# Both ends of layer 0: bias tables, loads, the last token chunk and the branch weights moved to other places in the order

## The chip, the cores and the metric

The kernel runs on one core of a Trainium2 chip. The metric is device microseconds of one execution. Before the change the median of three runs was 2273.14 us (2273.03 to 2274.25). The profiled execution spans 2274.0 us; all times inside it are counted from its start.

A core has a matrix engine (PE, with PEld for the loading of its weights), a vector engine (DVE), a scalar engine for activations and copies (ACT), a general engine (POOL) and a queue that mostly issues transfers (SP). ACT can issue transfers too; its queue then works through them in order, between its other instructions.

## The reference, cut to what matters

The input x has shape (2, 128, 64, 64) in float32: two images of 64 x 64 places with 128 channels. Layer 0 is a group norm, then a neighbourhood attention block: every place attends to a 7 x 7 window, in 4 heads, with a bias table per head, followed by a projection and a small chain of three linear maps with layer norms:

```python
x = x + _L0_conv_ref(_gn(x), ...)
t = _to_tokens(x)
t = t + _L1_attn_ref(_ln_t(t))
t = t + _L1_ffn_ref(_ln_t(t), sigma, phi, M_u, M_phi_plus, M_phi_minus, log_weights, gumbel)
```

Layer 1 is an attention of all 4096 tokens of an image with each other (the diagonal left out), and then a spectral filter: long causal convolutions in four branches of different length, of which a hard choice over `log_weights + gumbel` picks one. The chosen weights (`wt`, `seg`), a mixed matrix `mu` of short lags and the fourth root of `sigma` are small quantities that the filter needs only after most of the first attention.

## The kernel before, in words

**Layer 0, in bands.** The two images are cut into 16 bands of 8 rows (512 places), band k being image b, group g. A band's work is cut into named pieces: `p.*` (group norm `p.xg`, transposition to tokens `p.tok`, layer norm `p.bn` to `p.zT`, then `p.q`, `p.k`, `p.v` and their copies), four units `u0` to `u3` of the window attention (scores `S`, bias and row minimum `t`, exponential `e`, transposition `T`, copy `c`, product with the values `V`), `r.*` and `t.*` (the rest of the block), and `k.*`. The pieces `k.*` prepare the tokens of image 0 for layer 1 while image 1 is worked on: `k.a` transposes, `k.tt` copies, `k.bn` takes statistics, `k.pw` raises to the power -1/2, `k.z` normalizes on POOL, `k.b` and `k.cm` transpose back. Each band of image 1 handles one chunk of 512 tokens; the last band, k = 15, the last chunk.

**What sets the order.** `PLAN` gives each piece a time in a period of 2300 units, one period per band. All pieces, with the extra events for the tables and the weights, are sorted by that time and recorded in that order; inside `manual_schedule` the order of PE, DVE, ACT and POOL is kept as written. For the first two bands the preparing pieces follow the list `FIRST` instead, which also places the group norm (`gn`), the products for the q, k, v biases (`w`, kept by `wd`), the flips of the bias rows `f0` to `f3` (a PE product on the rows `rev`, and an ACT copy into `base`) and the tables (`tab` on POOL, `tab0` to `tab3` on DVE, each `mask` minus `base`). The queue of SP is not held to the written order.

**Loads at the start.** SP loads image 0 (`xa[0]`), the weights, the bias rows in 8 large pieces (ACT issues 8 small ones for head 0), the window masks, and image 1 (`xa[1]`). Between layer 0 and its attention, values go through memory: `p.vc` stores v to `vd`, and `windows` loads the windows `vw` back.

**Completion semaphores.** In the built program every transfer signals one of eight completion semaphores in turn, and an issue waits until an earlier user of the same semaphore has landed. The wait stands on the queue that issues.

**The end of layer 0 and the attention.** What the last bands have left when image 1's last unit is done is put into the list `later`. The program then enters layer 1: PSUM is handed over from layer 0's pools, `branch_weights` computes the choice, `mu` and the root of sigma, and `attention(0, fill)` begins. Its loop runs over pairs of token chunks; per pair it makes scores (`weights`: PE product, on the diagonal a DVE addition of `ndiag`, an ACT exponential), products `own` and `other`, and turned exponentials (`turned`). At every step it calls `fill()`, which takes one step from generators: first urgent ones (what follows a finished chunk), then, in order, `drain` (the list `later`, three pieces a step), `filters`, and `tokens` of image 1. Instructions of this part may be moved by the scheduler, as far as dependences and its own estimates allow.

Lines to follow below (as in the profile before): L188 transposes of z or of normalized tokens, L248/L252 flip and its copy, L257 tables, L326 transposes of xg or rb, L331 linear maps, L405 ACT's half of a normalization, L414 DVE's half, L435 xg, L459 kT, L508 scores, L521 bias and minimum, L531 exponentials, L544 transposes of them, L655 y, L661 relu of y on POOL, L705 the last step of a token chunk, L892/L899 scores and exponentials of the big attention, L920 own, L945 other, L1058 the root of sigma, L1096/L1098 `mu`.

Of the kernel before, what the change touches and what calls it, by code (L numbers as in the profile page):

```python
# [20 lines left out]
HEADS, DH, KW = 4, 32, 7  # L21
# [21 lines left out]
RPR = NTAB + 1  # L43
# [25 lines left out]
PERIOD = 2300  # L69


FIRST = (
    "gn p.xg0 p.xg1 p.tok0 p.tok1 w f0 p.bn0 p.bn1 f1 p.pw0 p.pw1 p.zd0 p.nb0 p.za0 p.tr0 f2 p.zd1 p.nb1 p.za1 p.tr1 f3"
    " wd p.zT0 tab p.v0 p.q0 p.k0 p.zT1 p.vc0 p.qT0 tab0 p.kT0 p.v1 p.k1 p.q1 p.vc1 p.kT1 p.qT1 tab1 tab2 tab3"
).split()
PHW = P + TH

# [15 lines left out]
def kernel(  # L93
# [16 lines left out]
    nc = tc.nc  # L110
# [12 lines left out]
    xa = [xp.tile([P, T], F32, tag=f"xa{b}", name=f"xa{b}") for b in range(NB)]  # L123
    xin = x.rearrange("b c h w -> b c (h w)")
    for c in range(4):
# [10 lines left out]
    mask = space[:, HEADS * NTAB * NTAB : HEADS * NTAB * NTAB + 6 * KEYS].rearrange("p (c k) -> p c k", k=KEYS)  # L136
# [8 lines left out]
        out=flip, in_=flip, compare_op=ALU.not_equal, fill=1.0, base=1 - QT * QT, pattern=[[0, 2], [1, QT * QT]],  # L145
# [73 lines left out]
    with l0a:  # L219
# [21 lines left out]
        tab = big.tile([P, 6, HEADS, KEYS], F32, name="tab")  # L241
# [38 lines left out]

        nc.gpsimd.memset(rev[:, 0].rearrange("p n m -> p (n m)"), 0.0)
        nc.gpsimd.memset(rev[:, HEADS - 1, NTAB], 0.0)
        for r in range(QT):
            lo = 6 - min(r, 6)
            src = bass.AP(
                rpb_pad.tensor, (RPR + r - 6) * RPW + 50, [[1, QT], [RPW, (HEADS - 1) * RPR - r // 7], [1, NTAB]]
            )
            rows_ = rev[r * QT : (r + 1) * QT].rearrange("p h n m -> p (h n) m")
            nc.sync.dma_start(out=rows_[:, RPR : HEADS * RPR - r // 7], in_=src)
            src = bass.AP(rpb_pad.tensor, (lo + r - 6) * RPW + 50, [[1, QT], [RPW, RPR - lo], [1, NTAB]])  # L290
            nc.scalar.dma_start(out=rows_[:, lo:RPR], in_=src)
        nc.sync.dma_start(out=mask, in_=nc.inline_tensor(_window_masks(), "window_masks").ap())
        wg = w_sb
        cb = wp.tile([P, 5], F32, name="cb")
        C_Q, C_K, C_V, C_1, C_3 = range(5)
# [174 lines left out]
        @piece("p.vc")  # L470
        def _(t, b, g):
            v = ap.tile([P, 4, P], F32, tag="v", name="v")
            nc.scalar.copy(v.rearrange("p j c -> p (j c)"), t["pv"])
            for i, c in enumerate(TILES):
                nc.sync.dma_start(
                    out=vd[b][g * QT : (g + 1) * QT, c * QT : (c + 1) * QT, :],
                    in_=v[(i % 2) * 64 : (i % 2 + 1) * 64, i // 2, :],
                )
            if b == 0 and g == 1:
                for c in range(4):  # L480
                    nc.sync.dma_start(out=xa[1][:, c * 1024 : (c + 1) * 1024], in_=xin[1, :, c * 1024 : (c + 1) * 1024])
            if g:
                windows(b, g - 1)
            if g == NG - 1:
                windows(b, g)
# [290 lines left out]
        for k, (b, g) in enumerate(order):  # L776
            t = {}
            for name, at in PLAN.items():
                if name[0] == "k" and b == 0:
                    continue  # L780

                at = FIRST.index(f"{name}{k}") - 1000 if k < 2 and name[0] == "p" else at + k * PERIOD
                events.append((at, k, name, lambda f=pieces[name], t=t, b=b, g=g: f(t, b, g)))
        for name, f in (
            ("gn", lambda: [None for _ in group_norm(0)]), ("w", weights), ("wd", weights_kept),
# [7 lines left out]
        rest_ = behind()  # L793
        for i in range(4):
            events.append((150 + 350 * i, None, "", lambda: next(rest_)))

        gn1 = group_norm(1)
        for i in range(7):
# [26 lines left out]
            for k, n in want:  # L825
                upto[k] = max(upto[k], rest(k, n))
        whole = [n == len(mine[k]) for k, n in enumerate(upto)]
        now, later = [], []
        for at, k, name, f in events:
            if name == "t.add":  # L830
                early = at <= last or whole[k]
            elif name[:1] in ("r", "t"):
                early = name in mine[k][: upto[k]]
            else:
                early = True
            (now if early else later).append(f)
        engines = mybir.EngineType
        with tc.manual_schedule(engines={engines.PE, engines.DVE, engines.Activation, engines.Pool}):
            for f in now:
# [12 lines left out]
    with ap_:  # L852
# [196 lines left out]
        def branch_weights():  # L1049

            lw = sp.tile([P, NBR], F32, tag="lw", name="lw")
            gu = sp.tile([P, NBR], F32, tag="gu", name="gu")
            nc.sync.dma_start(out=lw, in_=log_w.partition_broadcast(P))
            nc.sync.dma_start(out=gu, in_=gumbel.partition_broadcast(P))
            nc.sync.dma_start(out=sg, in_=sigma.partition_broadcast(P))
            quarter = sp.tile([P, KF], F32, tag="quarter", name="quarter")
            nc.gpsimd.memset(quarter, 0.25)
            nc.gpsimd.tensor_tensor(sg, sg, quarter, ALU.pow)  # L1058

            z = sp.tile([P, NBR], F32, tag="z", name="z")  # L1060
            nc.vector.tensor_tensor(z, lw, gu, ALU.add)
            m = sp.tile([P, 1], F32, tag="zm", name="zm")
            nc.vector.tensor_reduce(m, z, AX.X, ALU.max)
            nc.vector.tensor_scalar(z, z, m, None, ALU.subtract)
            ys = sp.tile([P, NBR], F32, tag="ys", name="ys")
            tot = sp.tile([P, 1], F32, tag="tot", name="tot")
            nc.scalar.activation(ys, z, AF.Exp, bias=0.0, scale=1.0, accum_out=tot)
            nc.vector.reciprocal(tot, tot)
            nc.vector.tensor_scalar(ys, ys, tot, None, ALU.mult)
            nc.vector.tensor_reduce(m, ys, AX.X, ALU.max)  # L1070

            oh = sp.tile([P, NBR], F32, tag="oh", name="oh")
            nc.vector.tensor_scalar(oh, ys, m, None, ALU.is_equal)
            seen = sp.tile([P, NBR], F32, tag="seen", name="seen")
            nc.vector.tensor_copy(seen[:, 0:1], oh[:, 0:1])  # L1075
            for i in range(1, NBR):
                nc.vector.tensor_tensor(seen[:, i : i + 1], seen[:, i - 1 : i], oh[:, i : i + 1], ALU.max)
            for i in range(NBR - 1, 0, -1):
                nc.vector.tensor_tensor(oh[:, i : i + 1], seen[:, i : i + 1], seen[:, i - 1 : i], ALU.subtract)

            for j in range(NBR):
                nc.vector.tensor_copy(seg[:, j : j + 1], seen[:, NBR - 1 - j : NBR - j])
            nc.vector.tensor_tensor(wt, oh, ys, ALU.subtract)
            nc.vector.tensor_tensor(wt, wt, ys, ALU.add)

            mixed(mu, m_u)

        def mixed(dst, src):
            dst2 = dst.rearrange("p k e -> p (k e)")
            for i in range(NBR):  # L1090
                st = sp.tile([P, 4, P], F32, tag="st", name="st")
                n = src.shape[1]
                nc.sync.dma_start(out=st[:, 0:n], in_=src[i].rearrange("k d e -> d k e"))
                st2 = st[:, 0:n].rearrange("p k e -> p (k e)")
                if i == 0:
                    nc.vector.tensor_scalar(dst2, st2, wt[:, 0:1], None, ALU.mult)  # L1096
                else:
                    nc.vector.scalar_tensor_tensor(dst2, st2, wt[:, i : i + 1], dst2, ALU.mult, ALU.add)  # L1098
# [83 lines left out]

            return fill, urgent

        branch_weights()
        def drain():

            rings[:] = [(ps_m, "bank")] * 2
            for i, f in enumerate(later):
                f()  # L1190
                if i % 3 == 2:
                    yield
            l0.close()
            tp1 = ap_.enter_context(tc.tile_pool(name="l1_t1", bufs=1, side="right"))
            tt[1] = tp1.tile([P, NT, P], F32, name="tt1")
            tok[1] = tp1.tile([P, NT, P], F32, name="tok1")
            cm[1] = tp1.tile([P, T], F32, name="cm1")
            yield

        steps = [drain(), filters(), tokens(1, bank)]  # L1200
        fill, left = filler(0, steps)
        attention(0, fill)
        for gen in steps:
# [156 lines left out]
def _window_masks():  # L1360

    import numpy as np

    def seen(offset):

        q, k = np.arange(QT)[:, None], np.arange(WN)[None, :]
        lo = np.clip(offset + q - 3, 0, WN - KW)
        return (k >= lo) & (k < lo + KW)

    m = np.zeros((2, QT, QT, 6, WN, WN), np.float32)  # L1370
    for ci in range(6):
        rows_ = seen((0, 6, 3)[ci // 2])
        for ab in range(2):
            cols = seen(((0, 6), (3, 3))[ci % 2][ab])
            m[ab, :, :, ci] = np.where(rows_[:, None, :, None] & cols[None, :, None, :], 0.0, -MASKED)
    return m.reshape(P, 6, KEYS)
# [77 lines left out]
```

## Time and profile before

| stretch (us) | what happens | PE busy | granted PE clock |
|---|---|---|---|
| 0 to 12 | image 0 loads, group statistics | 0.66 | 1.00 |
| 12 to 25 | first bands' norms, bias rows arrive | 7.50 | 1.00 |
| 25 to 44 | flips, v, q, k of two bands, tables | 14.22 | 1.00 |
| 44 to 60 | first scores of band 0 | 15.71 | 0.57 |
| 60 to 140 | bands in steady work | 74.53 | 0.98 |
| 140 to 260 | the same | 119.84 | 1.00 |
| 260 to 340 | the last bands of image 1 | 75.92 | 1.00 |
| 340 to 350 | the last units | 7.74 | 0.83 |
| 350 to 367 | hand-over to layer 1 | 9.74 | 0.70 |
| 367 to 377 | first products of attention 0 | 9.33 | 1.00 |
| 377 to 860 | attention 0 with fills | 472.23 | 1.00 |
| 860 to 900 | from attention 0 to 1 | 37.08 | 0.91 |
| 900 to 2274 | attention 1, convolution | 1349.48 | 0.99 |

PE is the engine that the whole program waits for: 96% of the span. A table row is to be read as follows: busy PE near the length of the stretch means that only less PE work would shorten it, and a gap means that PE waited for someone. The granted clock is the share of full speed that the throttle allowed; 0.5 is its low state.

In lines of the profile, each row is: start, busy time, engine, line, operation, tile written, tile read, shapes, number of instructions, and in brackets the idle time of the engine before it and what ended it. A float32 product shows as two PE records.

### The profile page before, as it was taken

Reading aid. Unit: us, or ns where it says so; the run is one execution under the profiler, and the core shown is the slowest. Engines: PE = TensorE matmul, PEld = TensorE weight load, DVE = VectorE, ACT = ScalarE, POOL = GpSimd, SP = SyncE. Lnnn points to the kernel's source line nnn. Section 1 sums busy time; section 2 is a strip of 40 time slices with the busy share of each in tenths; the row PEclk is TensorE's granted clock in tenths of the full one; section 3 lists DMA queues with packets and bytes.
Section 4 is the critical chain, followed back from the end, with each engine's and each line's share of the span. In section 5 each row is a group of like instructions: output and inputs, shape, how many; then the busy total and the mean of one; then the engine's idle time right before and its main releaser. Section 6 shows DMA issues by size and latency. Waiting matters only on the chain.

```text
span 2274.0 us, 31748 instructions
## 1 busy us (share of the span) xinstructions
PE 2194.0 (96%) x11908; PEld 1355.6 (60%) x11908; DVE 936.9 (41%) x3047; ACT 784.2 (34%) x1911; POOL 275.9 (12%) x354
## 2 busy tenths in 40 slices
PE   6999998999999999999999979999999999999998
PEld 3677764444444444544544436776776777767777
DVE  4799984333443336533333433222223232232323
ACT  2889883222332233222222223223223232232222
POOL 3377874200000000000000000000000000000000
PEclk8999998999999999999999989999999999999999
DMA  4222213021000015100000033222122121212101
GB/s 120 62 61 61 61 49 50 5 70 47 24 19 5 24 47 150 42 24 15 9 24 23 23 91 91 51 58 53 43 58 52 44 58 39 58 42 55 40 10 74
DMA packets 180858, 109.76 MB, mean 48 GB/s; under 512 B 32225, under 2 KB 165857, under 8 KB 180194
## 3 DMA queue, kind: packets, MB, share of 16 engines
q1 hardware_dynamic: 179466, 107.65, 18.4%
q8 instruction: 94, 1.54, 0.3%
q14 instruction: 58, 0.48, 0.1%
q10 hardware_dynamic: 1240, 0.09, 0.1%
HBM read 73.09 MB, written 34.60 MB: 47 GB/s over the span
## 4 chain that ended last, share of the span: by engine, by line
PE 86%; DVE 6%; POOL 4%; DMA 1%; ACT 1%; issue 1%; SPq 0%; POOLq 0%; DVEq 0%; ACTq 0%
PE acc L1278 25%; PE pc L1267 13%; PE own L920 10%; PE bank L892 9%; PE other L945 8%; PE bank L906 4%; PE bank L331 2%; PE py L1305 2%; PE bank L188 2%; PE bank L1037 2%; PE bank L544 2%; PE bank L1005 2%; PE bank L1141 1%; PE bank L508 1%; DVE ln_st L377 1%
## 5 line engine op out<-in xcount | busy, mean ns | idle before, releaser
L1268 DVE COPY y<-pc 128x512 f32<-128x512 f32 x320 | 221.6, 692 | 358.9 <-PE pc L1267 355.1
L899 ACT ACTIVATE e<-bank 128x512 f32<-128x512 f32 x288 | 171.8, 597 | 566.1 <-PE bank L892 434.1
L892 PE MATMUL bank<-cm 128*128 128x512 f32 x576 | 299.6, 604 | 3.9 <-DVE seen L1075 3.9
L1267 PE MATMUL pc<-ct,ut 64*128 64x512 f32 x1280 | 287.6, 599 | 5.9 <-issue 5.9
L1278 PE MATMUL acc<-y,mpl 128*128 128x256 f32 x1280 | 292.1, 382 | 0.0
L1278 PE MATMUL acc<-y,mmi 128*128 128x256 f32 x1280 | 288.0, 379 | 0.0
L1278 PEld LDWEIGHTS acc<-y,mpl 128*128 128x128 f32 x1280 | 238.1, 190 | 59.4 <-issue 29.6
L1278 PEld LDWEIGHTS acc<-y,mmi 128*128 128x128 f32 x1280 | 242.6, 190 | 32.7
L1268 ACT COPY y<-pc 128x512 f32<-128x512 f32 x320 | 204.3, 638 | 94.8 <-PE pc L1267 94.8
L920 PE MATMUL own<-et,tok 128*128 128x512 f32 x448 | 228.1, 596 | 3.5 <-DVE part L909 3.5
L945 PE MATMUL other<-e,tok 128*128 128x512 f32 x448 | 229.0, 593 | 0.9 <-DVE xa L959 0.9
L909 DVE CUSTOM_DVE_ANT_0 et<-bank,one 128x512 f32<-128x512 f32 x224 | 145.5, 688 | 166.9 <-PE bank L906 166.9
L1267 PEld LDWEIGHTS pc<-ct,ut 64*128 64x128 f32 x1280 | 121.9, 188 | 152.7 <-issue 147.5
L1284 ACT COPY ob<-acc 128x256 f32<-128x256 f32 x40 | 23.8, 595 | 431.2 <-PE acc L1278 431.2
L920 PEld LDWEIGHTS own<-et,tok 128*128 128x128 f32 x448 | 84.2, 190 | 112.5 <-issue 70.1
L945 PEld LDWEIGHTS other<-e,tok 128*128 128x128 f32 x448 | 85.3, 191 | 108.4 <-issue 106.7
L892 PEld LDWEIGHTS bank<-cm 128*128 128x128 f32 x576 | 96.8, 194 | 76.1 <-issue 47.0
L1317 DVE TENSOR_TENSOR xa<-py,xa 128x512 f32<-128x512 f32 x32 | 22.1, 691 | 281.4 <-PE py L1305 281.4
L906 PEld LDWEIGHTS bank<-ident,e 128*128 128x128 f32 x896 | 103.9, 142 | 55.3 <-issue 48.0
L160 POOL TENSOR_TENSOR ln_rs<-ln_rs,mhalf 128x4 f32<-128x4 f32 x24 | 24.3, 1012 | 878.2 <-DVE ln_rs L159 878.2
L531 ACT ACTIVATE p<-p,mn 128x196 f32<-128x196 f32 x256 | 114.4, 449 | 15.7 <-DVE mn L521 15.1
L906 PE MATMUL bank<-ident,e 128*128 128x128 f32 x896 | 117.5, 274 | 0.0
(200 smaller groups left out, 2340.5 us busy)
## 6 DMA issues: line engine op xcount, KB each, us to landing
ut<-us SPq DMA_DIRECT2D x80, 256.0 KB
us<-ub SPq DMA_DIRECT2D x64, 256.0 KB
vw<-vd SPq DMA_DIRECT2D x256, 49.0 KB
ct<-gs SPq DMA_DIRECT2D x160, 72.0 KB
ct<-gs SPq DMA_DIRECT2D x160, 64.0 KB
gs<-ub SPq DMA_DIRECT2D x20, 256.0 KB
xa<-in_x_dram SPq DMA_DIRECT2D x8, 512.0 KB
vd<-v SPq DMA_DIRECT2D x128, 32.0 KB
```

Source lines behind the costliest of these rows:

```text
L188: nc.tensor.transpose(ps[:, j * P : (j + 1) * P], src[:, j, :], ident)
L331: nc.tensor.matmul(pl, lhsT=wg[:, lo : lo + P], rhs=zT, start=True, stop=True)
L531: nc.scalar.activation(p, p, AF.Exp, bias=t[name + "mn"][:, h : h + 1], scale=-1.0, accum_out=t["den"][:, u, h : h + 1],)
L892: nc.tensor.matmul(ps, lhsT=cm[b][:, n * P : (n + 1) * P], rhs=cm[b][:, chunk(c)], start=True, stop=True)
L899: nc.scalar.activation(e, ps, AF.Exp, bias=0.0, scale=ASCALE, accum_out=part[:, n, c : c + 1])
L906: nc.tensor.transpose(pt[:, k * P : (k + 1) * P], es[k][:, m * P : (m + 1) * P], ident)
L909: nc.vector.tensor_tensor_reduce(et, pt, one, 1.0, 0.0, ALU.mult, ALU.add, part[:, n, a : a + 1])
L920: nc.tensor.matmul(own, lhsT=tok[b][:, n, :], rhs=e, start=first, stop=last)
L945: nc.tensor.matmul(other, lhsT=tok[b][:, 4 * CHUNKS[a] + j, :], rhs=es[j], start=(j == 0), stop=(j == 3))
L1267: nc.tensor.matmul(pc, lhsT=ut[fp, b, par, :], rhs=cv_[fp], start=True, stop=True)
L1268: (nc.scalar.copy if f else nc.vector.tensor_copy)(y[:, 4 * f : 4 * f + 4, :, par, b * 2 * FB + q : (b + 1) * 2 * FB : 2], pc.rearrange("p ...
L1278: nc.tensor.matmul(acc, lhsT=(mmi if l else mpl)[:, k, :], rhs=y[:, 1::2, k, ::-1, :] if l else y[:, 0::2, k, :, :], start=(l == 0 and k = ...
```

## The change: what it does and what it is for

It has four parts.

1. **Written order of the start.** `FIRST` is rewritten: both bands' normalizations come before the bias flips, `f0` follows `p.zT0`, `f1` follows `p.tr1`, `f2` and `f3` come after band 0's q, k, v, and POOL's tables after these. `p.xg2` is put into the list early. The placing rule now takes every name in `FIRST`, not only the first two bands.
2. **Loads of the start.** The masks are loaded ahead of the bias rows; two of the eight large pieces of bias rows (r = 2 and 5) are issued by ACT. The load of image 1 leaves SP's queue: ACT issues its four pieces, as an event at time 1000 of band 0, so that they keep out of the bias rows' way.
3. **The last chunk of tokens.** The `k` pieces of the last band are taken out of the written order and put at the head of `later`, so that they become steps between the attention's products.
4. **Branch weights.** `branch_weights` becomes a generator with `yield`s: its first loads are issued where it stood, and the rest are steps of the fill, after `drain`.

The arithmetic is the same before and after.

```diff
--- before.py
+++ after.py
@@ -70,8 +70,8 @@
 
 
 FIRST = (
-    "gn p.xg0 p.xg1 p.tok0 p.tok1 w f0 p.bn0 p.bn1 f1 p.pw0 p.pw1 p.zd0 p.nb0 p.za0 p.tr0 f2 p.zd1 p.nb1 p.za1 p.tr1 f3"
-    " wd p.zT0 tab p.v0 p.q0 p.k0 p.zT1 p.vc0 p.qT0 tab0 p.kT0 p.v1 p.k1 p.q1 p.vc1 p.kT1 p.qT1 tab1 tab2 tab3"
+    "gn p.xg0 p.xg1 p.tok0 p.tok1 w p.bn0 p.bn1 p.pw0 p.pw1 p.zd0 p.nb0 p.za0 p.tr0 p.zd1 p.nb1 p.za1 wd p.xg2 p.zT0 f0"
+    " p.tr1 f1 p.v0 p.q0 p.k0 p.zT1 p.vc0 p.qT0 tab0 p.kT0 f2 f3 tab p.v1 p.k1 p.q1 tab1 p.vc1 p.kT1 p.qT1 tab2 tab3"
 ).split()
 PHW = P + TH
 
@@ -280,16 +280,16 @@
 
         nc.gpsimd.memset(rev[:, 0].rearrange("p n m -> p (n m)"), 0.0)
         nc.gpsimd.memset(rev[:, HEADS - 1, NTAB], 0.0)
+        nc.sync.dma_start(out=mask, in_=nc.inline_tensor(_window_masks(), "window_masks").ap())
         for r in range(QT):
             lo = 6 - min(r, 6)
             src = bass.AP(
                 rpb_pad.tensor, (RPR + r - 6) * RPW + 50, [[1, QT], [RPW, (HEADS - 1) * RPR - r // 7], [1, NTAB]]
             )
             rows_ = rev[r * QT : (r + 1) * QT].rearrange("p h n m -> p (h n) m")
-            nc.sync.dma_start(out=rows_[:, RPR : HEADS * RPR - r // 7], in_=src)
+            (nc.scalar if r % 3 == 2 else nc.sync).dma_start(out=rows_[:, RPR : HEADS * RPR - r // 7], in_=src)
             src = bass.AP(rpb_pad.tensor, (lo + r - 6) * RPW + 50, [[1, QT], [RPW, RPR - lo], [1, NTAB]])
             nc.scalar.dma_start(out=rows_[:, lo:RPR], in_=src)
-        nc.sync.dma_start(out=mask, in_=nc.inline_tensor(_window_masks(), "window_masks").ap())
         wg = w_sb
         cb = wp.tile([P, 5], F32, name="cb")
         C_Q, C_K, C_V, C_1, C_3 = range(5)
@@ -476,9 +476,6 @@
                     out=vd[b][g * QT : (g + 1) * QT, c * QT : (c + 1) * QT, :],
                     in_=v[(i % 2) * 64 : (i % 2 + 1) * 64, i // 2, :],
                 )
-            if b == 0 and g == 1:
-                for c in range(4):
-                    nc.sync.dma_start(out=xa[1][:, c * 1024 : (c + 1) * 1024], in_=xin[1, :, c * 1024 : (c + 1) * 1024])
             if g:
                 windows(b, g - 1)
             if g == NG - 1:
@@ -779,7 +776,7 @@
                 if name[0] == "k" and b == 0:
                     continue
 
-                at = FIRST.index(f"{name}{k}") - 1000 if k < 2 and name[0] == "p" else at + k * PERIOD
+                at = FIRST.index(f"{name}{k}") - 1000 if f"{name}{k}" in FIRST else at + k * PERIOD
                 events.append((at, k, name, lambda f=pieces[name], t=t, b=b, g=g: f(t, b, g)))
         for name, f in (
             ("gn", lambda: [None for _ in group_norm(0)]), ("w", weights), ("wd", weights_kept),
@@ -793,6 +790,11 @@
         rest_ = behind()
         for i in range(4):
             events.append((150 + 350 * i, None, "", lambda: next(rest_)))
+        def second():
+            for c in range(4):
+                nc.scalar.dma_start(out=xa[1][:, c * 1024 : (c + 1) * 1024], in_=xin[1, :, c * 1024 : (c + 1) * 1024])
+
+        events.append((1000, None, "", second))
 
         gn1 = group_norm(1)
         for i in range(7):
@@ -825,7 +827,8 @@
             for k, n in want:
                 upto[k] = max(upto[k], rest(k, n))
         whole = [n == len(mine[k]) for k, n in enumerate(upto)]
-        now, later = [], []
+
+        now, later, chunk_ = [], [], []
         for at, k, name, f in events:
             if name == "t.add":
                 early = at <= last or whole[k]
@@ -833,7 +836,8 @@
                 early = name in mine[k][: upto[k]]
             else:
                 early = True
-            (now if early else later).append(f)
+            (chunk_ if name[:1] == "k" and k == bands[-1] else now if early else later).append(f)
+        later = [*chunk_, *later]
         engines = mybir.EngineType
         with tc.manual_schedule(engines={engines.PE, engines.DVE, engines.Activation, engines.Pool}):
             for f in now:
@@ -1053,6 +1057,7 @@
             nc.sync.dma_start(out=lw, in_=log_w.partition_broadcast(P))
             nc.sync.dma_start(out=gu, in_=gumbel.partition_broadcast(P))
             nc.sync.dma_start(out=sg, in_=sigma.partition_broadcast(P))
+            yield
             quarter = sp.tile([P, KF], F32, tag="quarter", name="quarter")
             nc.gpsimd.memset(quarter, 0.25)
             nc.gpsimd.tensor_tensor(sg, sg, quarter, ALU.pow)
@@ -1067,6 +1072,7 @@
             nc.scalar.activation(ys, z, AF.Exp, bias=0.0, scale=1.0, accum_out=tot)
             nc.vector.reciprocal(tot, tot)
             nc.vector.tensor_scalar(ys, ys, tot, None, ALU.mult)
+            yield
             nc.vector.tensor_reduce(m, ys, AX.X, ALU.max)
 
             oh = sp.tile([P, NBR], F32, tag="oh", name="oh")
@@ -1077,13 +1083,16 @@
                 nc.vector.tensor_tensor(seen[:, i : i + 1], seen[:, i - 1 : i], oh[:, i : i + 1], ALU.max)
             for i in range(NBR - 1, 0, -1):
                 nc.vector.tensor_tensor(oh[:, i : i + 1], seen[:, i : i + 1], seen[:, i - 1 : i], ALU.subtract)
+            yield
 
             for j in range(NBR):
                 nc.vector.tensor_copy(seg[:, j : j + 1], seen[:, NBR - 1 - j : NBR - j])
             nc.vector.tensor_tensor(wt, oh, ys, ALU.subtract)
             nc.vector.tensor_tensor(wt, wt, ys, ALU.add)
 
+            yield
             mixed(mu, m_u)
+            yield
 
         def mixed(dst, src):
             dst2 = dst.rearrange("p k e -> p (k e)")
@@ -1182,7 +1191,6 @@
 
             return fill, urgent
 
-        branch_weights()
         def drain():
 
             rings[:] = [(ps_m, "bank")] * 2
@@ -1197,7 +1205,9 @@
             cm[1] = tp1.tile([P, T], F32, name="cm1")
             yield
 
-        steps = [drain(), filters(), tokens(1, bank)]
+        chosen = branch_weights()
+        next(chosen)
+        steps = [drain(), chosen, filters(), tokens(1, bank)]
         fill, left = filler(0, steps)
         attention(0, fill)
         for gen in steps:
```

## The prediction

> **What bounds the kernel now.** I read the page first, then busy time by stretch, then the instructions in order of time at the two ends of layer 0, and last the two programs' built orders.
>
> ```profile
> PE 2194.0 (96%) x11908; PEld 1355.6 (60%) x11908; DVE 936.9 (41%) x3047; ACT 784.2 (34%) x1911; POOL 275.9 (12%) x354
> ```
>
> PE (TensorE) is busy for 96% of 2274.0 us, so 80 us is all that any reordering could win. In the table by stretch (columns: stretch, sum, busy time of PE, weight loads, DVE, ACT, POOL, then granted clock, DMA share, GB/s) PE is full in the middle and loose at the ends:
>
> ```profile
> 12.00:25.00 13.00, 7.50 (x22) 4.81 (x22) 6.90 (x33) 2.56 (x5) 4.07 (x7) 1.00 0.97 154
> 25.00:44.00 19.00, 14.22 (x40) 7.50 (x40) 4.54 (x12) 5.63 (x12) 8.19 (x15) 1.00 0.23 74
> 140.00:260.00 120.00, 119.84 (x1844) 88.48 (x1843) 114.08 (x592) 107.53 (x332) 94.56 (x116) 1.00 0.22 61
> 350.00:367.00 17.00, 9.74 (x23) 5.08 (x24) 7.53 (x39) 2.43 (x8) 13.96 (x15) 0.70 0.00 0
> ```
>
> From 12 to 44 PE idles 10.3 us, from 350 to 367 7.3 us; after that it loses little. What is gained at an end stays, because the middle is bound by PE's own work. At the start:
>
> ```profile
> 22.50 1.67 PE L248 MATMUL bank<-cm,flip 64*128 64x400 f32 x2 [3.38 <-DMA cm<-in_rpb_pad_dram]
> 24.21 0.49 ACT L252 COPY tok<-bank 128x400 f32<-128x400 f32 x1 [4.56 <-PE bank L248]
> 24.60 0.81 ACT L405 ACTIVATE z<-bank,ln_nb,ln_rs 128x128 f32<-128x128 f32 x2
> 25.12 1.25 PE L188 MATMUL bank<-ident,z 128*128 128x128 f32 x4 [0.94 <-ACT z L405]
> 43.30 0.94 PE L326 MATMUL bank<-ident,xg 128*128 128x128 f32 x4 [2.59 <-DVE xg L435]
> 44.17 0.70 PE L508 MATMUL bank<-kT,qT 32*64 32x196 f32 x16
> ```
>
> The bias rows land late; flip f1 waits for them, its ACT copy waits for f1, and behind that copy on the in-order ACT queue stands band 0's normalization (24.60), whose input (ln_nb) was ready at 18.55. The first scores come at 44.17. At the seam:
>
> ```profile
> 349.36 3.15 POOL L705 TENSOR_SCALAR tok<-tt,kmv,krs 128x128 f32<-128x128 f32 x4
> 353.44 1.51 POOL L661 TENSOR_SCALAR y<-y 128x512 f32<-128x512 f32 x1
> 354.98 0.30 DVE L377 BATCH_NORM_STATS2 ln_st<-y 128x6 f32<-128x128 f32 x1 [6.99 <-POOL y L661]
> 357.39 1.12 DVE L655 SCALAR_TENSOR_TENSOR y<-bank,ln_rs,add 128x128 f32<-128x128 f32 x4
> 358.66 6.16 PE L892 MATMUL bank<-cm 128*128 128x512 f32 x10 [3.92 <-DVE seen L1075]
> 359.02 2.93 POOL L1058 TENSOR_TENSOR sg<-sg,quarter 128x16 f32<-128x16 f32 x1
> 362.96 0.41 DVE L394 SCALAR_TENSOR_TENSOR ln_nb<-ln_mv,ln_rs 128x4 f32<-128x4 f32 x1 [4.38 <-POOL ln_rs L385]
> 366.73 1.12 PE L920 MATMUL own<-e,tok 128*128 128x512 f32 x2 [1.91 <-ACT e L899]
> ```
>
> POOL's last token chunk (3.15) holds y, DVE's statistics of y hold L655, the last reader of layer 0's PSUM, and the attention's first products wait for that. Then the power of sigma (2.93) holds POOL's ln_rs, DVE stands 4.38, and the diagonal and exponentials come late.
>
> **What the skill says.** "DMA: Bandwidth & Descriptors", Issuing engines are not separate DMA queues: transfers started by ACT and SP share the engines, so another issuer saves only issue time; Anatomy of one DMA puts any semaphore wait on the issuing sequencer. The trace agrees: SP stood 4.6 us before a bias load for v_sb's landing. "ScalarE: Activation LUTs", What ACT_TABLE_LOAD costs: 1283 ns for the load; here 1.28 (at 12.02). "TensorE: Matmul & The Clock Gate", Part 1: half clock after about 3.4 us of idling. The trace agrees in kind: from 350 to 367 the granted clock was 0.70.
>
> **The start.** The built order gives ACT both za before any copy, but the table load now stands at za0 with its wait, so 18.55 + 1.28 + 0.81 puts tr0 at 20.7 instead of 25.12. PE then has tr0 1.25, f0 1.64, tr1 1.25, f1 1.64: v0 at 26.5 instead of 32.89. The bias rows should land in time for f1 (24.9): they landed at 22.4 by the trace's completion events, and the mask now goes ahead of them (588 KB, about 1.4 us by the 1.28 us between landings of 512 KB chunks). v0 to q1 took 7.8 us, f2 and f3 between them add 3.3: at these half-clock durations k1 ends near 36.8, at the durations of the warm stretch near 33.0. Then kT1 0.88, two tables 1.45 (two of the four now come earlier), statistics 1.18: first score reduction at 36.4 to 40.3 instead of 45.36. I take **7.0 us earlier**. xg of band 2 (0.73) lies in DVE's idle time before kT, POOL's tables beside PE; both cost nothing.
>
> **The cost of moving xa[1].** Its four issues move from SP at 18.44, where nothing waited, to ACT, in the built order right behind band 2's za (52.88) and ahead of unit 1's exponentials (53.66). Issuing is 4 x 0.43 = 1.7 us, but each also waits for an earlier transfer that used its completion semaphore: the built program makes them wait for the 4th, 8th and 12th window load (vw), and the fourth for the second xa piece. SP starts the window loads at 45.59, one each 0.77, landing 2.5 after the issue; moved up by the same 7 the 12th lands at 49.7, while ACT gets there at 46.7. The second piece, issued near 46.7 and landing 3 to 4 later (the first load took 4.0), frees the fourth at 50 to 51. So ACT stands about 4.3 us, with 1.7 (no waits) and 6 as bounds. Queued behind are unit 1's four exponentials, and unit 1's transposes on PE (55.97) need them: 4.0 of it shows. PE idling that long would also go to half clock for a window or so: 1.2 (0 to 2). About 0.4 comes back in PE's 5.5 idle us from 60 to 140. Start, net: 7.0 - 4.0 - 1.2 + 0.4 = **2.2 us gained**.
>
> **The seam.** POOL loses krs and the 3.15; y is ready at 351.8 instead of 354.95. In the built order y's statistics and ln_nb also stand no longer ahead of L655, which then only needs PE's w2, freed from behind the token transposes (350.5): L655 ends near 351.8, the attention's first products start near 352.0 instead of 358.66. Sigma's power moves behind ln_rs, so nothing holds the diagonals; the first own product follows the five products, near 356.4 (warm) to 358.6 (half clock) instead of 366.73. But the last chunk now stands early among the products: its transposes (k.b) come four products after k.a, and their input needs ACT's copy, DVE's statistics (behind mu, which waits for m_u's last pieces, 2.55 us after issue), then POOL: sigma 2.93, y 1.50, krs 1.27, tok 4 x 0.79. By my count tok is ready from 361.9 to 364.2 while PE is there at 360.2: a **new wait of about 3 to 4 us**. PE then reaches the end of the fourth own product (373.74 before) at 367.9, 5.8 earlier; 1.3 off for half clock gives **4.5** (bounds 2 and 9.5, without the wait). The other branch steps are tiny DVE operations beside PE. The chunk's two PE groups (0.88) only change place. Fills: in the built order batch 1's tokens still end inside attention 0, a few steps later, so nothing is left exposed after it.
>
> **Sum:** 2273.1 - 2.2 - 4.5 = 2266.4; I take 2266.5.
>
> **Rivals.** (A) As above, both ends pay in part: 2266.5, chance 0.53 (0.44 of it beyond 0.2%). (B) The ACT wait is absorbed and the token wait hidden: 7.0 + 9.5 less half a microsecond, about 2257; for it, ACT is busy only half of 44 to 60; against it, both waits are in the built order. 0.18. (C) One end gives everything back, for instance the ACT wait and half clock take all of the 7.0 and the seam keeps 2: about 2271, no difference. For it, the trace's clock drops after each hole. 0.19. (D) Slower: ACT stands 6 and PE runs 2 longer on half clock against a start gain of only 5 (loss 3), and at the seam the token wait exceeds what is won: 2276 or more. Against it, the removed waits are large and certain. 0.10.
>
> **Numbers.** The range 2256.5 to 2273.5 leaves out the better half of B and D, 0.19. Faster 0.44 + 0.18 = 0.62; same 0.09 + 0.19 = 0.28; slower 0.10.
>
> **What would show it.** First scores near 35 to 38; ACT idle before unit 1's exponentials, put down to DMA; first attention product near 352 less what the start won; PE waiting for tok on POOL inside the first four own products. Wrong would be: ACT going through its issues in 2 us, no tok wait, the first bias flips waiting on DMA again (mask ahead of the rows), or idle time at the end of attention 0 (820 to 880) growing.

## The result and the profile after

The changed kernel takes 2264.5 us (median of four runs, 2263.27 to 2266.85), the kernel before 2273.55 us beside it: a ratio of 0.9961, 95% interval 0.9944 to 0.9978, so 9 us or 0.4% faster. The predicted time was 2266.5. The profiled execution spans 2263.3 us. Lines of the start and the seam have numbers lower by 3 in this kernel (L505 is L508 of before), those of the attention higher by 4 (L896 is L892). Busy time and instructions by engine:

```profile
PE 2187.7 (97%) x11908; PEld 1354.1 (60%) x11908; DVE 940.2 (42%) x3047; ACT 785.3 (35%) x1911; POOL 277.3 (12%) x354
```

PE's busy time fell from 2194.0 to 2187.7 with the same 11908 products, which is less time at half clock (PE was busy for 64.2 us at half clock before and for 53.2 after); the rest of the gain is idle time. So the 80 us of idle time were not all that a reordering could win, as the prediction took them to be. The granted clock of 1.00 in the first rows, before and after, is no measurement: the first clock record of the traces stands at 37.7 us before and at 30.1 after. Until then products take the times of half clock (the eight records of a value product, L465, 2.08 us at 32.89 before and 1.05 at 37.94), and the two sums at half clock count them so. Where the gain went is read from the table by stretch (columns as before):

```profile
12.00:25.00 13.00, 8.76 (x30) 6.04 (x30) 7.54 (x35) 3.87 (x7) 3.85 (x6) 1.00 0.44 25
25.00:44.00 19.00, 16.10 (x72) 9.95 (x70) 8.66 (x33) 6.50 (x16) 11.69 (x19) 0.90 0.16 40
44.00:60.00 16.00, 9.57 (x82) 5.60 (x80) 5.27 (x26) 6.46 (x22) 0.53 (x1) 0.50 0.56 180
140.00:260.00 120.00, 119.84 (x1846) 88.76 (x1845) 114.30 (x597) 108.00 (x333) 94.10 (x115) 1.00 0.22 61
350.00:367.00 17.00, 11.85 (x36) 5.68 (x37) 11.20 (x49) 4.75 (x16) 16.72 (x18) 0.93 0.57 65
377.00:860.00 483.00, 476.62 (x1581) 233.96 (x1579) 191.29 (x641) 136.24 (x346) 30.30 (x33) 1.00 0.10 33
```

The stretch from 25 to 44 is fuller (14.22 before), but from 44 to 60 PE is busy for 9.57 us instead of 15.71, all of it at half clock: what the start won is lost there. The half clock itself is older than the hole: it begins at 40.4, behind a wait of 2.90 us for DVE (L759, at 39.89), as it began at 44.5 in the kernel before behind one of 2.59. The hand-over gained 2.1, and from 377 to 860, a stretch that the prediction left alone, PE is busy for 4.4 us more (472.23 before), which is idle time gone.

**The start came as drawn, and then a hole opened.** In order of time, PE and then ACT in the kernel after:

```profile
20.28 1.25 PE L188 MATMUL bank<-ident,z 128*128 128x128 f32 x4 [2.95 <-ACT z L405]
...
25.76 2.08 PE L465 MATMUL bank<-w_sb,zT 128*128 128x128 f32 x8
...
35.47 0.59 PE L505 MATMUL bank<-kT,qT 32*64 32x196 f32 x16
```

```profile
45.92 0.37 ACTq L795 DMA_DIRECT2D xa<-in_x_dram  x1
46.23 0.45 ACT L405 ACTIVATE z<-bank,ln_nb,ln_rs 128x128 f32<-128x128 f32 x1
47.02 6.89 ACTq L795 DMA_DIRECT2D xa<-in_x_dram  x3
53.95 0.46 ACT L528 ACTIVATE p<-p,mn 128x196 f32<-128x196 f32 x1 [7.28 <-DMA vw<-vd]
```

The first scores come 8.7 us earlier (44.17 before), the first score reduction at 38.67 instead of 45.36. But ACT's sequencer (ACTq) needs 6.89 us for its last three issues, and unit 1's exponentials stand behind them. PE reaches that unit's transposes at 55.43, after 6.27 us of idling; before it was there at 55.97. Half clock, which lasts to 60.9 (58.2 before), then takes the rest: a linear map of the last bands (L331), close ahead of the seam, starts at 341.61, where it started at 341.06 before. **Net: 0.5 us lost.**

**The seam and what follows.** PE in the kernel after, with the wait that the last token chunk brings:

```profile
353.51 4.53 PE L896 MATMUL bank<-cm 128*128 128x512 f32 x10 [1.38 <-DVE y L652]
357.88 1.02 PE L924 MATMUL own<-e,tok 128*128 128x512 f32 x2
...
364.56 0.44 PE L188 MATMUL bank<-ident,tok 128*128 128x128 f32 x1 [2.63 <-POOL tok L702]
365.36 0.47 PE L188 MATMUL bank<-ident,tok 128*128 128x128 f32 x1 [0.37 <-POOL tok L702]
366.18 0.47 PE L188 MATMUL bank<-ident,tok 128*128 128x128 f32 x1 [0.35 <-POOL tok L702]
366.96 0.47 PE L188 MATMUL bank<-ident,tok 128*128 128x128 f32 x1 [0.30 <-POOL tok L702]
367.23 1.92 PE L896 MATMUL bank<-cm 128*128 128x512 f32 x2
```

The last line shows a second price of such a wait: a pair of records that takes 1.02 at full clock takes 1.92 behind it. The clock was 0.50 from 364.6 to 371.5.

To compare both kernels over equal work, take the stretch from the linear map just named to the transposes of the first finished chunks (L969 before, L973 after; at 589.7 and 581.5). By line, the same products lie in it, except that eight of image 1's token transposes (at 570 and 583 before) come only behind it in the kernel after, at 603 and 616. Before:

```profile
341.05:589.70 248.65, 235.86 (x805) 120.15 (x806) 96.24 (x336) 65.13 (x172) 38.78 (x46) 0.97 0.16 39
```

After:

```profile
341.60:581.48 239.88, 233.47 (x797) 119.95 (x798) 93.85 (x318) 63.83 (x170) 38.80 (x44) 0.97 0.16 41
```

It is 8.8 us shorter: 6.4 of less idle time (12.79 to 6.41) and 2.4 of less busy time. About 0.9 of that is the eight transposes, which are only put off, so some 7.9 us are gained. Less than half of the idle time was saved at the hand-over; the other 3.6 us are holes of the kernel before between 376 and 436 (0.67, 2.11 and 0.86), which are gone. The two large ones, in order of time in the kernel before:

```profile
409.68 1.50 POOL L661 TENSOR_SCALAR y<-y 128x512 f32<-128x512 f32 x1
411.21 0.87 DVE L377 BATCH_NORM_STATS2 ln_st<-y 128x6 f32<-128x128 f32 x4 [4.43 <-POOL y L661]
412.00 0.67 DVE L909 CUSTOM_DVE_ANT_0 et<-bank,one 128x512 f32<-128x512 f32 x1
412.74 1.70 PE L920 MATMUL own<-et,tok 128*128 128x512 f32 x2 [2.11 <-DVE part L909]
...
435.05 1.12 PE L945 MATMUL other<-e,tok 128*128 128x512 f32 x2 [0.86 <-DVE xa L959]
```

A leftover piece of layer 0 (statistics of y) stands on DVE ahead of the attention's turned exponentials and waits 4.43 us for POOL's relu; the own product needs those exponentials and PE idles 2.11. Then the clock is 0.50 from 413.2 to 416.6, some 1.7 us more. In the kernel after, PE waits for nothing from 373 to 476. The two profiled executions differ by 10.7 us, more than the medians (9.0); of that, 2.4 lie behind this stretch, most of it between 845 and 885, where PE waits 2.92 us before and 1.89 after and half clock lasts 6.8 and 3.4. That wait differs among the runs (2.89 with part 3 alone), so nothing is built on it here.

### The profile page after: what moved, and what is told of

Read it like the earlier page. It is cut to its first block, busy times and chain, and to the rows that moved or that the text cites. A ratio compares the mean times of both kernels' runs of the same rounds, so it can differ in the third digit from the quotient of the medians.

```text
span 2263.3 us, 31741 instructions
## 1 busy us (share of the span) xinstructions
PE 2187.7 (97%) x11908; PEld 1354.1 (60%) x11908; DVE 940.2 (42%) x3047; ACT 785.3 (35%) x1911; POOL 277.3 (12%) x354
## 4 chain that ended last, share of the span: by engine, by line
PE 87%; DVE 5%; POOL 3%; DMA 1%; ACT 1%; issue 1%; SPq 1%; POOLq 0%; DVEq 0%; ACTq 0%
PE acc L1288 25%; PE pc L1277 13%; PE bank L896 10%; PE own L924 10%; PE other L949 8%; PE bank L910 4%; PE bank L331 2%; PE py L1315 2%; PE bank L188 2%; PE bank L1041 2%; PE bank L1009 2%; PE bank L541 1%; PE bank L1150 1%; PE po L563 1%; PE bank L505 1%
## 5 line engine op out<-in xcount | busy, mean ns | idle before, releaser
L896 PE MATMUL bank<-cm 128*128 128x512 f32 x576 | 298.4, 602 | 1.4 <-DVE y L652 1.4
L896 PEld LDWEIGHTS bank<-cm 128*128 128x128 f32 x576 | 96.4, 193 | 72.4 <-issue 44.5
```

Source lines behind the costliest of these rows:

```text
L896: nc.tensor.matmul(ps, lhsT=cm[b][:, n * P : (n + 1) * P], rhs=cm[b][:, chunk(c)], start=True, stop=True)
```

## The experiments

Each ratio is to the kernel before, timed beside it, with its 95% interval.

### The two ends apart

The start alone (parts 1 and 2 of the diff, the seam as before):

> Parts 1 and 2 of the change alone (order of the start, its loads, image 1 issued by ACT); the seam as before. Theory T (the 8.7 us by which the first scores come earlier are all taken back by the 7.3 us that ACT stands at the image-1 loads and by half clock; the whole gain is made at the seam and in the fills behind it): no gain, 2273.0 to 2275.0, PE at the seam's last zT product (341.06 before) at 341 to 342. Rival R1 (the start keeps 2.2 us as predicted): 2271.3. Rival R3 (a shifted start changes which holes open later, so the two ends do not add): outside both, below 2270 or above 2276.

Measured: 2273.31 us, ratio 0.9996 (0.9988 to 1.0004). ACT stands 7.98 us, PE waits 6.98 before unit 1's transposes, the linear map at the seam starts at 341.62. T holds: the start as written gains nothing that these times show.

The seam alone (parts 3 and 4):

> Parts 3 and 4 alone (last token chunk at the head of the later list, branch weights as steps); the start as before. T: carries all of the gain, 2263.3 to 2265.0. R1 (start keeps 2.2, seam 6.8): 2266.7. R3: above 2268, the seam's gain hangs on the state in which the start leaves the queues.

Measured: 2263.35 us, ratio 0.9961 (0.9948 to 0.9973), the ratio of the whole change. T holds; all of the gain comes from the seam's parts.

### What the move of image 1 costs

```diff
-                nc.scalar.dma_start(out=xa[1][:, c * 1024 : (c + 1) * 1024], in_=xin[1, :, c * 1024 : (c + 1) * 1024])
+                nc.sync.dma_start(out=xa[1][:, c * 1024 : (c + 1) * 1024], in_=xin[1, :, c * 1024 : (c + 1) * 1024])
```

> The whole change, but image 1's four loads are issued by SP (right behind the bias rows) and not by ACT. T: ACT stands no longer (7.28 us after), the first transposes of unit 1 come at 47 to 49 in place of 55.43 and the half clock behind the hole goes: 2257 to 2259. R2 (the middle or the later bands absorb an earlier start; or image 1's 2 MB now delay v's stores and windows by as much): 2263 to 2265. R4 (2 MB beside the bias rows hold up f1 again): 2260 to 2262, PE waiting for DMA at a bias flip.

Measured: 2258.47 us, ratio 0.9937 (0.9924 to 0.9949): 6.0 us less than the change as written, as T has it. The stretch by stretch table of this kernel:

```profile
25.00:44.00 19.00, 16.11 (x69) 9.65 (x68) 8.96 (x34) 6.49 (x16) 11.53 (x20) 0.92 0.16 37
44.00:60.00 16.00, 15.62 (x213) 10.71 (x211) 10.00 (x52) 11.40 (x38) 2.38 (x3) 0.78 0.23 66
```

The stretch from 44 to 60 has 213 PE records where the change as written has 82. The bias flips wait for no DMA, so R4 falls too. SP issues the four pieces from 17.23 on and is done with them long before it has a window to load. The linear map at the seam starts at 334.61 (341.61 as written), so nearly all of it is kept. The edit changes the issuing queue and the time of issue at once (17.2 instead of 45.9); what the queue alone is worth, with the pieces issued at 45.9 by SP, no run shows.

Why ACT stood 7.28 us and not the 4.3 of the prediction:

```diff
-                nc.scalar.dma_start(out=xa[1][:, c * 1024 : (c + 1) * 1024], in_=xin[1, :, c * 1024 : (c + 1) * 1024])
+                lo = c * 1024
+                nc.scalar.dma_start(out=xa[1][:, lo : lo + 256], in_=xin[1, :, lo : lo + 256])
...
+            if b == 0 and g == 1:
+                for c in range(4):
+                    lo, hi = c * 1024 + 256, (c + 1) * 1024
+                    nc.sync.dma_start(out=xa[1][:, lo:hi], in_=xin[1, :, lo:hi])
```

> The whole change, but ACT issues only the first 256 of each 1024 columns of image 1 (four issues of 128 KB at the same place in ACT's queue, each still waiting for an earlier window load's semaphore); the other three quarters go out on SP at the start. Theory H1 (ACT stood 7.3 us and not 4.3 because each 512 KB piece itself delays the window loads whose landing the next issue waits for: 2.5 us rose to 5 or 6): window loads land in 2.5 to 3.5 us, ACT stands 2.5 to 4 us, 2259 to 2262. Rival H2 (the semaphore waits alone make the hold, size does not matter): ACT stands 6 to 8 us, 2263 to 2265. Rival H3 (any hold at this place opens the hole and the half clock): ACT stands 3 us and the time is still above 2263.

Measured: 2259.52 us, ratio 0.9937 (0.9925 to 0.9950). ACT in this kernel:

```profile
46.63 0.36 ACTq L800 DMA_DIRECT2D xa<-in_x_dram  x1
...
47.03 3.85 ACTq L800 DMA_DIRECT2D xa<-in_x_dram  x3
50.94 0.46 ACT L532 ACTIVATE p<-p,mn 128x196 f32<-128x196 f32 x1 [3.55 <-DMA xa<-in_x_dram]
```

The stand of 3.55 us is in H1's range. By the trace's completion events a window load (49 KB) landed 2.5 us after its issue until the first 512 KB piece was issued, then 3.9 to 6 us after it; beside 128 KB pieces 2.3 to 3.5. Each piece thus prolonged the very transfers that the next issue waited for. One caveat: the built program gives the small pieces other partners (their issues wait for the 4th, 6th, 8th and 10th window load; in the change for the 4th, 8th and 12th, and the fourth for the second piece). The 12th window load landed at 51.64 in this kernel. An estimate from this: had the third issue waited for it as in the change, ACT would have stood until about 52.5, some 5.1 us. So about 2.2 of the 3.7 us come from the size of the pieces and 1.5 from the partners, and the size is only the larger part of the cause. PE waited 2.55 here instead of 6.27, and by the median times all but about 1 of the 6 us were back: H3 falls. The profiled execution, the slowest of the five (2262.07), shows less of it: it reaches the linear map at the seam at 340.62, after a wait of 0.91 for a window load at 218 and half clock from 318 to 325.

### What the start's parts are worth without that

The start with image 1 on SP, the seam as before (parts 1 and 2 with the edit above):

> Parts 1 and 2 with image 1 issued by SP, the seam as before. Theory T (without the stand of ACT the start is worth what the whole change gained by the same edit, 6.0 us, and the two ends add): 2266.7 to 2268.2. Rival R3 (the ends do not add; an earlier start meets another hand-over with its own holes): above 2269 or below 2265.

Measured: 2266.58 us, ratio 0.9968 (0.9956 to 0.9980). T holds. Start 0.32% and seam 0.39% make 0.71%, and both together gave 0.63% (0.51 to 0.76): the ends add, within the intervals.

The new order alone (`FIRST` and the line that places it), with every load as in the kernel before:

> Part 1 alone: the new written order of the start; masks, bias rows and image 1 are loaded as in the kernel before. Theory L1 (the loads were moved for nothing: with the new order f0 and f1 come at 22 to 25 us, when the rows, landed at 22.4, are there already): as with parts 1 and 2 and SP, 2266.5 to 2269. Rival L2 (masks and image 1 ahead of the tables' rows matter: PE waits for DMA at a flip, or tables wait for the mask that lands at 23.65): 2270 to 2272.

Measured: 2266.89 us, ratio 0.9968 (0.9955 to 0.9980), the same ratio. L1 holds: PE waits for no DMA at a flip although the bias rows are loaded as before. Part 2 of the change brings nothing that these times show, and with image 1 on ACT it costs the start's whole gain.

### Which part of the seam

The last chunk alone (part 3):

> Part 3 alone: the last token chunk goes to the head of the later list; start and branch weights as before. T, sum of the two halves: the chunk frees POOL (3.15 us) ahead of relu y, but the power of sigma (2.9 us) still holds the diagonal, so about half, 2268 to 2270. R5 (the shift of the later list by the chunk's pieces is what closes the holes at 412 and 435, and sigma's place matters little): 2264.5 to 2266. R6 (the chunk alone only trades one wait for another, the branch steps carry the gain): 2272 to 2274.

Measured: 2264.43 us, ratio 0.9962 (0.9950 to 0.9975). My theory of halves fell; part 3 carries everything. POOL at its hand-over shows why sigma's place did not need part 4:

```profile
349.89 1.50 POOL L661 TENSOR_SCALAR y<-y 128x512 f32<-128x512 f32 x1
...
353.54 1.55 POOL L639 TENSOR_TENSOR x<-x,xa 128x128 f32<-128x128 f32 x2
355.05 3.24 POOL L1060 TENSOR_TENSOR sg<-sg,quarter 128x16 f32<-128x16 f32 x1
358.28 1.74 POOL L661 TENSOR_SCALAR y<-y 128x512 f32<-128x512 f32 x1
```

This part of the program may be reordered, and with the chunk gone the scheduler itself put the power of sigma behind the sums of x. The next ln_rs still stands behind that power, at 364.63, but it holds no diagonal: the last of these ends at 355.91. The statistics of y, which stood ahead of the diagonals before (354.98), come behind them here (359.63).

The branch weights alone (part 4):

> Part 4 alone: the branch weights as steps of the fill; start, last chunk and pace of the later list as before. In the built order the power of sigma then stands behind the ln_rs that it held up, and the chooser's small DVE steps no longer stand between the statistics of y and the diagonals, but the last chunk still holds POOL for 3.15 us ahead of relu y. Theory B1 (what part 4 takes away, the 2.9 us of sigma and the 4.38 us stand of DVE, is hidden behind the wait for y or turns into another wait): 2272 to 2274. Rival B2 (it is worth what the prediction ascribed to it, the exponentials 2 to 3 us earlier): 2269.5 to 2271.5.

Measured: 2274.31 us, ratio 1.0004 (0.9995 to 1.0012). B1 holds (its range ended at 2274). DVE still waits 7.04 us for the relu of y behind the chunk. Then the normalization of y, which stood behind L655 before, stands ahead of it on DVE, and PE waits longer for L655:

```profile
357.88 0.16 DVE L394 SCALAR_TENSOR_TENSOR ln_nb<-ln_mv,ln_rs 128x4 f32<-128x4 f32 x1 [0.83 <-POOL ln_rs L385]
357.96 0.91 DVE L414 TENSOR_SCALAR z<-y,ln_mv,ln_rs 128x128 f32<-128x128 f32 x2
...
358.86 1.12 DVE L655 SCALAR_TENSOR_TENSOR y<-bank,ln_rs,add 128x128 f32<-128x128 f32 x4
...
360.12 7.30 PE L892 MATMUL bank<-cm 128*128 128x512 f32 x10 [5.09 <-DVE zm L1064]
```

Before, these products started at 358.66. The view puts the wait down to zm, a step of the choice that ends at about the same time; but the products start 0.14 us after the end of L655, as they do in the kernel after (353.37 and 353.51).

**How much of part 3 is the chunk, how much the pace?** Put at the head of `later`, its seven pieces push all others 2 1/3 fill steps back. First that push alone, with the chunk where it was:

```diff
-            for i, f in enumerate(later):
-                f()
+            for i, f in enumerate([*[None] * 7, *later]):
+                if f:
+                    f()
```

> The kernel before, with nothing moved but the pace of the later list: seven empty places stand ahead of its pieces, so that each comes 2 1/3 fill steps later among the attention's products, as behind the last chunk's seven pieces in the change; the last chunk itself and the branch weights stay as before. Theory S1 (that shift alone closes the two holes at 412 and 435 us, 2.1 and 0.9 us with the half clock behind the first worth 1.7): 2268 to 2269.5, no PE wait above 0.7 us from 400 to 440. Rival S2 (the holes close because the hand-over runs earlier, not by the shift): 2272.5 to 2274.5, holes still there.

Measured: 2271.35 us, ratio 0.9988 (0.9982 to 0.9995). Neither expectation. The holes at 412 and 435 are gone, as S1 has it, but the gain is about half of S1's, and another hole opened; PE waits in this kernel between 375 and 480:

```profile
382.03 2.07 PE L920 MATMUL own<-et,tok 128*128 128x512 f32 x2 [2.54 <-DVE part L909]
```

Here the statistics and normalization of the first leftover piece meet the first turned exponentials on DVE. Then the chunk beside the other pieces, which keep their steps (`ahead` holds the chunk's pieces):

```diff
-            for i, f in enumerate(later):
-                f()
+            ahead = list(chunk_)
+            for i, f in enumerate(later):
+                if ahead:
+                    ahead.pop(0)()
+                f()
```

> Part 3 without the shift: the last token chunk leaves the written order, and its seven pieces are recorded one each beside the first seven pieces of the later list, which keep their steps; the rest as before. S1: half of the gain, 2267.5 to 2270, with holes near 412 and 435 still there (a little earlier). S2: 2263.5 to 2265.5, as with the chunk at the list's head.

Measured: 2270.2 us (2263.94 to 2274.15), ratio 0.9985 (0.9979 to 0.9992). The hand-over starts early (first products at 352.10), and the old holes are there:

```profile
408.33 1.13 PE L921 MATMUL own<-et,tok 128*128 128x512 f32 x2 [2.10 <-DVE part L910]
...
430.64 1.13 PE L946 MATMUL other<-e,tok 128*128 128x512 f32 x2 [0.85 <-DVE xa L960]
```

S1 is right on the holes: moving the chunk does not close them, the pace does. The two halves make 0.12% and 0.15%; together they give 0.38%. A part of what is missing is the hole at 382, which appears with the pace alone and not with both. PE's idle time from 340 to 377 is 6.6 us in this kernel and was 10.2 before, which is about the size of the 0.15% (3.4 us). The granted clock was higher there too (0.91, and 0.82 before); but single times of this kernel scatter by 10 us, so what half clock adds is not resolved.

### Without the wait for the chunk

Image 1 on SP, and other leftover pieces between the chunk's statistics and its scaling:

```diff
-        later = [*chunk_, *later]
+        later = [*chunk_[:4], *later[:12], *chunk_[4:], *later[12:]]
```

> The change with image 1 loaded by SP, and in the later list twelve pieces between the last chunk's statistics and its scaling and transposes, so that ten more products stand ahead of these on PE. Theory G1 (the wait for tok, 2.6 and three times 0.35 us, and the half clock behind it are real losses of the change at the seam): 4 to 7 us below the same without the gap (2258.5), 2251.5 to 2254.5, no wait for tok. Rival G2 (another wait takes its place, such as the exponentials or normalized inputs of the next pieces): 2257 to 2259.

Measured: 2253.86 us, ratio 0.9910 (0.9894 to 0.9926), against 0.9937 (0.9924 to 0.9949) without the gap: some 5 to 6 us by these, in G1's range, though the intervals touch; the profile shows it plainly. From 344 to 375 PE waits in this kernel only here:

```profile
344.50 4.53 PE L896 MATMUL bank<-cm 128*128 128x512 f32 x10 [1.38 <-DVE y L652]
360.82 0.55 PE L188 MATMUL bank<-ident,z 128*128 128x128 f32 x3 [0.63 <-ACT z L405]
364.38 1.12 PE L896 MATMUL bank<-cm 128*128 128x512 f32 x2 [1.71 <-ACT e L903]
```

The granted clock is 1.00 from 350 to 377. A little of G2 is there (0.63 and 1.71), and the clock did not fall behind it. This is the fastest kernel of the study. The same without part 4:

> The best version so far (order of the start, image 1 by SP, twelve pieces between the last chunk's statistics and its scaling) without part 4. Theory P1 (part 4 carries nothing measurable, as the last chunk alone gave the same as the chunk with it): 2253 to 2255.5, not to be told from 2253.9. Rival P2 (with the chunk's wait gone, the branch weights on DVE between the first products show): 2256 to 2259.

Measured: 2254.69 us, ratio 0.9914 (0.9901 to 0.9928). P1 holds: part 4 is not to be told from nothing here either.

## Why the prediction was right, and where its steps were wrong

The time was 2 us off, but two of its terms were wrong by more, in opposite directions. That the number came out so well is luck in good part: the errors nearly cancel. None of the four signs that it named for being wrong came; PE's idle time from 820 to 880, the last of them, went from 6.4 to 5.4 us.

- **The start, 7.0 us earlier: right.** tr0 at 20.28 (predicted 20.7), v0 at 25.76 (26.5), first score reduction 6.7 us earlier. Its reason was the order; the loads that the prediction let arrive "in time for f1" by the mask's and the rows' new places arrive in time with the old places too (order alone, 0.9968).
- **"So ACT stands about 4.3 us", bounds 1.7 to 6: mis-sized.** The mechanism (issues that wait for semaphores of window loads, exponentials behind them) was right, the term measured 7.28, outside the bounds. The working let window loads land 2.5 us after issue, as in the trace of before, and the second piece 3 to 4 after; with the pieces under way these were 3.9 to 6 and 5.6. The 12th window load, for which the third issue waits, was issued at 47.62 and landed at 53.06 instead of 49.7. The prediction quoted the Trainium skill, "DMA: Bandwidth & Descriptors", Issuing engines are not separate DMA queues, for saying that ACT's and SP's transfers share the engines, and then took the latencies as if they did not.
- **The start's net, "2.2 us gained": wrong**, by that term; measured 0.5 lost, and the start alone 0.9996. The 0.4 that was to come back did not.
- **The first products near 352.0, the first own product at 356.4 to 358.6:** 353.51 and 357.88. The first is 1.5 late, as the seam was reached 0.5 later and half clock lasted 6.8 us there (340.8 to 347.6) instead of 3.4.
- **The wait for tok, 3 to 4 us: right.** 2.63, 0.37, 0.35 and 0.30 make 3.65.
- **The end of the fourth own product at 367.9, and from it 4.5 for the seam: wrong as a measure.** That product ends near 372.8, some 1 us earlier than before, because half clock lasted 6.8 us behind the wait (1.3 was allowed) and because other pieces now stand ahead of it. At equal work the seam and what follows are worth 7.9 us in these two profiles, and the seam alone is worth 8.9 by its ratio (0.9961).
- **The fills, "so nothing is left exposed after it": the step that failed most.** Nothing was exposed at the end, as it says, but it looked only at whether the fills end inside attention 0, and not at the 2.11, 0.86 and 0.67 us that PE waited in the kernel before inside the fills, which a change of the list's pace moved (in the push alone two of them closed and one of 2.54 opened). More than half of the idle time saved at the seam comes from there.
- **"Sigma's power moves behind ln_rs, so nothing holds the diagonals": wrong cause.** In the kernel after, sigma's power (357.22) still stands ahead of the next ln_rs (367.20). What freed the diagonals is that y's statistics, and with them the wait for that ln_rs, went behind them (361.89) when the chunk left. With part 4 alone sigma's power does move behind ln_rs (359.39 and 356.81), and that is worth nothing (1.0004).

So rival A's number came true by a start smaller by 2.7 and a seam (with its fills) larger by 4 to 5 than its terms. Of rival C ("the ACT wait and half clock take all of the 7.0") the first half came true. Rival B's 9.5 for the seam is near the measured 8.9, but not for its reason: the token wait was not hidden.

## What to carry to other kernels

A transfer's latency, read from a quiet trace, is not its latency beside large transfers that the same change puts there; where an in-order compute queue waits for it, take the loaded figure, or issue the large transfer early, from a queue that nobody waits for. When work is pushed into or out of a list that is drained a few pieces a step, look at every hole the list makes now, far beyond the edit: the pace itself is a change. And when a change has several parts, time each alone: here one part carried the gain, one was neutral, and one undid another's gain, which was nearly as large (0.32% against 0.39%).

## What the runs showed of the hardware that I had not expected

- 49 KB loads took 2.5 us to land alone, 2.3 to 3.5 beside 128 KB transfers and 3.9 to 6.8 beside 512 KB transfers of another issuing engine (6.8 in the run with the start alone).
- The length of a hole of PE did not tell whether half clock followed. Behind one of 2.11 us (412.74 before) the clock was 0.50 for 3.4 us, and behind one of 2.63 and three of 0.3 to 0.4 (364.56 after) for 6.8. Behind one of 2.59 us (855.99 in the fastest kernel) it stayed at 1.00. The same wait of 1.60 us for DVE's z (L177) was followed by half clock in the kernel after (848.12), and not in the kernel before (857.05). "The trace's clock drops after each hole", as the prediction has it, is too much: behind 1.91 us (366.73 before) it stayed at 1.00. The Trainium skill, "TensorE: Matmul & The Clock Gate", Part 1, speaks of an idle window of about 3.4 us; the holes that were followed by half clock here are shorter. At the hand-over of the kernel before, too, the clock fell at 351.7, ahead of the long hole (3.92 us) and behind four of 0.45 to 0.74.
- The power of a 128x16 tile took POOL 2.93 to 3.25 us, of a 128x4 tile 1.01 to 1.04.
